# Mixture of experts on tokens sorted by expert: row tiles of 128 with indirect scatter and gather in place of all experts on all tokens

## Chip, cores and metric

The kernel runs on one core of a Trainium2 chip. The metric is the device time of one execution in microseconds; the time given is the median of three runs.

## What is computed

The input is 16 sequences of 256 tokens, 128 wide, in f32. Four stages follow one another, each on the layer-normalised output of the one before, each with a residual: attention a (causal, 8 heads, a geometric term in the scores), experts (called B), attention b (16 heads, not causal), and the experts again (called D, with the same weights). The experts:

```python
logits = einsum('bsd,ed->bse', tgt, Wr) + br          # 8 experts
top_v, top_i = top_k(logits, 2)
top_w = softmax(top_v)
router_w = sum(one_hot(top_i, 8) * top_w[..., None], axis=-2)
h = relu(einsum('bsd,efd->bsef', tgt, W1) + b1)       # F = 512
o = einsum('bsef,edf->bsed', h, W2) + b2
tgt2 = einsum('bsed,bse->bsd', o, router_w)
return layer_norm(tgt + tgt2, gamma, beta)
```

Only two of the eight weights of a token are not zero.

## The kernel before

The 4096 tokens are cut into 8 groups of 512 (two sequences, four tiles of 128 tokens). For each group there is one stage of each kind: A (attention a), B (experts), C (attention b), D (experts). The program is unrolled in Python. `attention` returns a list of steps, small functions that each issue a few instructions; `experts` returns another.

An attention normalises its group (`layernorm`, with DVE statistics and a power step on POOL, L179 and L180), turns it (`transposed`, L191), projects q and k (L230) and v (L245), then goes through units of four heads and one sequence. A unit computes scores with the queries on the partitions (`maxima`, L265), takes the row maxima on DVE (L275, L280), turns them (`shift`, L291), computes the scores again with the keys on the partitions (`weights`, L309), takes the exponential on ACT (L319), and multiplies with v (`weighted`, L328). The heads of a unit lie on 32 partitions each, so the score matmuls use 32 rows of the PE array each.

An expert stage normalises and turns its group into `tgtT` (128 x 512). `route` computes the logits (L427) and the two weights of each token. `spread` turns the weights, writes them to DRAM and reads them back onto every partition (L481, L485). Then all 8 experts run on all 512 tokens: `up` (L497) makes one quarter of the hidden layer, 128 x 512 in PSUM, ACT or DVE applies bias and relu (L506, L504), and `down` (L513) adds four such quarters up. DVE multiplies an expert's output with its weights (L522), and POOL adds it to the sum (L527). `end` turns the sum back (L532), `end2` normalises, scales and adds the residual on POOL (L541 to L547). The weights of all experts are loaded once at the start (16 loads of 256 KB) and stay.

Two streams of stages are interleaved in the program: A0, A1, C0, A2, C1 and so on, and B0, B1, D0, B2, D1 and so on. A stage opens when the stage before it on the same group is done. The attention stream goes ahead while it is at most 1.25 stages in front. So except at both ends an attention always has an expert stage of another group beside it. A scheduler below the program assigns buffers and orders the instructions of each engine, with the order in the program as priority; the engines then run their queues in order. All loads and stores go through SP's queue.

Of the kernel before, what the change touches and what calls it, by code (L numbers as in the profile page):

```python
# [9 lines left out]
F32 = mybir.dt.float32  # L10
AF = mybir.ActivationFunctionType
# [6 lines left out]
T = 256          # tokens of one batch element  # L18
C = 128          # model width
G = 512          # tokens of one group: two batch elements  # L20
NT = G // P      # token tiles of a group
HA, DA = 8, 16   # heads and head width of the first attention
HB, DB = 16, 8   # and of the second
E, F = 8, 512    # experts and their hidden width
NF = F // P
EB = 4          # experts whose token weights are spread in one load
EPS = 1e-5
NEG = -1e30
# columns of the constants
C_DD, C_ID, C_KA, C_KB, C_DESC, C_N = 0, 256, 512, 513, 514, 522  # L30
# [3 lines left out]
def block_kernel(  # L34
    ctx: ExitStack,
    tc: tile.TileContext,
    x: bass.AP,        # [tokens, C]
    wqT_a: bass.AP,    # [C out, C in]
    wk_a: bass.AP,     # [C in, C out]
    wv_a: bass.AP,     # [C in, C out]  # L40
    wo_a: bass.AP,     # [C in, C out]
    hs: bass.AP,       # [C, 1] head scale of each q column
    wq_b: bass.AP,     # [C in, C out]
    wk_b: bass.AP,
    wv_b: bass.AP,
    wr: bass.AP,       # [C, E]
    br: bass.AP,       # [E]
    w1: bass.AP,       # [C, E, F]
    b1: bass.AP,       # [P, E, NF]
    w2: bass.AP,       # [P, E, NF, C]  # L50
    b2: bass.AP,       # [C, E]
    gamma: bass.AP,    # [C]
    beta: bass.AP,     # [C]
    cst: bass.AP,      # [P, C_N]
    out: bass.AP,      # [tokens, C]
# [37 lines left out]
    b1_sb = loaded("b1_sb", b1)  # L93
    b2_sb = loaded("b2_sb", b2)
    w1_sb, w2_sb = [], []
    for e in range(E):
        w1_sb.append(loaded(f"w1_{e}", w1[:, e, :]))
        w2_sb.append(loaded(f"w2_{e}", w2[:, e, :, :]))
# [20 lines left out]
    )  # L119
    mhalf = const.tile([P, NT], F32, name="mhalf")  # L120
    nc.gpsimd.memset(mhalf, -0.5)

    # Each head takes 32 partitions of q^T and k^T, so that four heads lie in the four row
    # groups of the PE array. The row behind a head's own is 1 in k^T, and takes minus the
    # row maximum of the scores in q^T.
    # first attention: q' = q (scale I + head_scale d d^T), folded into its weights
# [22 lines left out]
    # v with a column of ones behind each head's, for the row sums  # L149
# [9 lines left out]
    # minus the row maxima, token-major, one column of 32 for a head  # L159
# [10 lines left out]
    def layernorm(src, dst, n):  # L170
        """dst = (src - mean) / sqrt(var + eps) over the last axis of [P, NT, C]."""
        st = small.tile([P, NT, 6], F32, tag="st", name=f"st_{n}")
        mv = small.tile([P, NT, 2], F32, tag="mv", name=f"mv_{n}")
        for t in range(NT):
            nc.vector.bn_stats(st[:, t, :], src[:, t, :])
        for t in range(NT):
            nc.vector.bn_aggr(mv[:, t, :], st[:, t, :])
        r = small.tile([P, NT], F32, tag="lnr", name=f"lnr_{n}")
        nc.gpsimd.tensor_scalar(r, mv[:, :, 1], EPS, None, ALU.add)  # L179
        nc.gpsimd.tensor_tensor(r, r, mhalf, ALU.pow)  # L180
        for t in range(NT):
            nc.vector.tensor_scalar(
                dst[:, t, :], src[:, t, :], mv[:, t, 0:1], r[:, t:t + 1],
                ALU.subtract, ALU.mult,
            )

    def transposed(src, dst, n):
        """[P tokens, NT, C] -> [C, G]"""
# [5 lines left out]
    def mask_diagonals(ps, mask):  # L194
        """The blocks at columns 0 and 256 of both heads are on the diagonal."""
# [8 lines left out]
    def attention(kind, g):  # L204
        """The steps of an attention and its residual on group g."""
# [48 lines left out]
        def maxima(bb, quad, pair, u):  # L254
            """Scores with the queries on the partitions, for their row maxima."""
# [4 lines left out]
            # (query tile, columns, keys)  # L260
# [25 lines left out]
        def shift(bb, quad, u):  # L286
            """q^T with minus the row maxima behind each head."""
# [11 lines left out]
        def weights(bb, quad, pair, u):  # L299
            """exp(scores - maxima) with the keys on the partitions."""  # L300
# [3 lines left out]
            # (key tile, columns, first query)  # L304
# [17 lines left out]
        def weighted(bb, quad, u):  # L322
            """(weights v)^T, and their sums behind each head."""
# [85 lines left out]
    def experts(n, g, last):  # L409
        """The steps of the mixture of experts, its norm and its residual on group g."""  # L410
        s = {}

        def start():
            tgt = work.tile([P, NT, C], F32, tag="tgt", name=f"tgt_{n}")
            layernorm(xg[g], tgt, n)
            s["tgt"] = tgt

        def start2():
            tgtT = work.tile([P, G], F32, tag="tgtT", name=f"tgtT_{n}")
            transposed(s["tgt"], tgtT, n)  # L420
            s["tgtT"] = tgtT

        def route():
            """The weights of the two best experts of each token; the first of equals wins."""
            ps = ps_mm.tile([P, NT, E], F32, tag="mm", name=f"lg_{n}")
# [6 lines left out]
            desc = cst_sb[:, C_DESC:C_DESC + E].unsqueeze(1).to_broadcast(shape)  # L432

            def best(lg, i):
                m = small.tile([P, NT], F32, tag=f"rm{i}", name=f"rm{i}_{n}")
                nc.vector.tensor_reduce(m, lg, axis=AX.X, op=ALU.max)
                eq = small.tile(shape, F32, tag="req", name=f"req{i}_{n}")
# [4 lines left out]
                k = small.tile([P, NT], F32, tag="rk", name=f"rk{i}_{n}")  # L442
                nc.vector.tensor_reduce(k, eq, axis=AX.X, op=ALU.max)
                one = small.tile(shape, F32, tag=f"rone{i}", name=f"rone{i}_{n}")
# [5 lines left out]
            lg = small.tile(shape, F32, tag="rl", name=f"rl_{n}")  # L450
# [3 lines left out]
            m1, one1 = best(lg, 1)  # L454
            lg2 = small.tile(shape, F32, tag="rl2", name=f"rl2_{n}")
# [3 lines left out]
            m2, one2 = best(lg2, 2)  # L459
            ex = small.tile([P, NT], F32, tag="rex", name=f"rex_{n}")  # L460
            nc.vector.tensor_tensor(ex, m2, m1, ALU.subtract)
            nc.scalar.activation(ex, ex, AF.Exp)
            wa = small.tile([P, NT], F32, tag="rwa", name=f"rwa_{n}")
            nc.vector.tensor_scalar(wa, ex, 1.0, None, ALU.add)
            nc.vector.reciprocal(wa, wa)
            wb = small.tile([P, NT], F32, tag="rwb", name=f"rwb_{n}")
            nc.vector.tensor_tensor(wb, ex, wa, ALU.mult)
            w = small.tile([P, E, NT], F32, tag="rw", name=f"rw_{n}")
            nc.vector.tensor_tensor(one1, one1, wa.unsqueeze(2).to_broadcast(shape), ALU.mult)
            nc.vector.tensor_tensor(one2, one2, wb.unsqueeze(2).to_broadcast(shape), ALU.mult)  # L470
            nc.vector.tensor_tensor(w.rearrange("p e t -> p t e"), one1, one2, ALU.add)
            s["w"] = w

        def spread():
            """The weights with the tokens on the free axis, on every partition."""
            ps = ps_mm.tile([E * NT, P], F32, tag="mm", name=f"wt_{n}")
            nc.tensor.transpose(ps, s["w"].rearrange("p e t -> p (e t)"), ident)
            wT = small.tile([E * NT, P], F32, tag="wT", name=f"wT_{n}")
            nc.vector.tensor_copy(wT, ps)
            wd = dpool.tile([E * NT, P], F32, tag="wd", name=f"wd_{n}")  # L480
            nc.sync.dma_start(out=wd, in_=wT)  # L481
            s["wbc"] = []
            for i in range(E // EB):
                wbc = work.tile([P, EB, G], F32, tag="wbc", name=f"wbc_{n}_{i}", bufs=3)
                nc.sync.dma_start(  # L485
                    out=wbc.rearrange("p e k -> p (e k)"),
                    in_=wd[i * EB * NT:(i + 1) * EB * NT, :]
                    .rearrange("a b -> (a b)").partition_broadcast(P),
                )
                s["wbc"].append(wbc)  # L490

        hs_ = {}

        def up(i):
            e, f = divmod(i, NF)
            ps = ps_h.tile([P, G], F32, tag="h", name=f"h_{n}_{i}")
            nc.tensor.matmul(  # L497
                ps, lhsT=w1_sb[e][:, f * P:(f + 1) * P], rhs=s["tgtT"],
                start=True, stop=True,
            )  # L500
            hT = work.tile([P, G], F32, tag="hT", name=f"hT_{n}_{i}", bufs=4)
            bias = b1_sb[:, e, f:f + 1]
            if f == NF - 1:
                nc.vector.tensor_scalar(hT, ps, bias, 0.0, ALU.add, ALU.max)  # L504
            else:
                nc.scalar.activation(hT, ps, AF.Relu, bias=bias)  # L506
            hs_[i] = hT

        def down(i):
            e, f = divmod(i, NF)  # L510
            if f == 0:
                s["o"] = ps_mm.tile([P, G], F32, tag="mm", name=f"o_{n}_{e}")
            nc.tensor.matmul(  # L513
                s["o"], lhsT=w2_sb[e][:, f, :], rhs=hs_.pop(i),
                start=(f == 0), stop=(f == NF - 1),
            )
            if f < NF - 1:
                return
            if e == 0:
# [148 lines left out]
```

## Time and profile before

| | |
|---|---|
| median of 3 runs | 1953.25 us (1953.03 to 1953.45) |
| profiled execution, first to last instruction | 1953.5 us |
| granted TensorE clock, mean | 0.903 |
| busy: PE, DVE, ACT, POOL | 1775.6, 824.6, 494.1, 279.3 us |
| HBM read, written | 40.73 MB, 2.36 MB |
| DMA queue of SP | 43.10 MB, 6.0% of 16 engines' span |

The page of the profile gives each engine's busy time and its share of the span, a strip of 40 equal slices, the DMA queues, the chain of work that ended last, and the costliest groups of instructions. A group's line has the source line, the engine, the operation, output and inputs, shapes, the count, busy time in us and the mean ns of one, then the idle time of the engine ahead of these instructions and what ended it. Matmuls overlap in the records, so the mean duration of one is longer than the distance from one start to the next. PE's clock is given as a share of full speed. The chain that ended last is 85% PE, 7% DVE and 7% POOL.

### The profile page before, as it was taken

The numbers are of one execution on the slowest core, as the hardware profiler recorded it, in microseconds if no ns is written. First come the engines' busy times: TensorE is split into PE (matmuls) and PEld (weight loads), VectorE is DVE, ScalarE is ACT, GpSimd is POOL, SyncE is SP. The second block draws the span as 40 slices with busy tenths as digits, with TensorE's granted clock in tenths as the row PEclk, the third lists the DMA queues.
The fourth block names the chain that finished last, engine by engine and source line by source line (L and its number), as shares of the span: only waits on it lengthen the run. The fifth ranks groups of instructions, "written<-read, shape, count | busy, mean of one in ns | idle before, by whom it ended". The sixth has DMA issues, their size and how long they took to land.

```text
span 1953.5 us, 19448 instructions
## 1 busy us (share of the span) xinstructions
PE 1775.6 (91%) x7794; PEld 848.6 (43%) x7794; DVE 824.6 (42%) x1912; ACT 494.1 (25%) x705; POOL 279.3 (14%) x293
## 2 busy tenths in 40 slices
PE   7896998989989899798998989899998989969977
PEld 4443444444444444344444434444444444434433
DVE  5444335453354533545335453454435453243232
ACT  1130231313313133131322223132231313303311
POOL 1012002120121201212011110211102120120122
PEclk7697898999979799798998989899897999979978
DMA  4010100101010010101001010010100101001010
GB/s 148 1 43 1 44 1 0 44 6 44 1 44 1 6 44 1 44 1 49 2 1 44 1 49 1 1 44 1 49 1 1 44 6 44 1 1 44 1 49 5
DMA packets 18377, 44.33 MB, mean 23 GB/s; under 512 B 2160, under 2 KB 12016, under 8 KB 14192
## 3 DMA queue, kind: packets, MB, share of 16 engines
q1 hardware_dynamic: 18288, 43.10, 6.0%
q8 instruction: 61, 1.00, 0.2%
q14 instruction: 28, 0.23, 0.0%
HBM read 40.73 MB, written 2.36 MB: 22 GB/s over the span
## 4 chain that ended last, share of the span: by engine, by line
PE 85%; DVE 7%; POOL 7%; issue 1%; SPq 0%; DMA 0%; POOLq 0%; ACT 0%; DVEq 0%
PE h_B L497 13%; PE o_B L513 13%; PE h_D L497 12%; PE o_D L513 11%; PE st_b L309 7%; PE s_b L265 7%; PE av_b L328 4%; PE pj_b L230 3%; PE st_a L309 3%; PE s_a L265 2%; PE pj_a L230 2%; PE av_a L328 2%; POOL x L547 1%; PE ot_b L372 1%; PE lg_D L427 1%
## 5 line engine op out<-in xcount | busy, mean ns | idle before, releaser
L497 PE MATMUL h_B<-tgtT_B,w 128*128 128x512 f32 x512 | 288.5, 654 | 0.2 <-DVE tgtT_B L192 0.2
L497 PE MATMUL h_D<-tgtT_D,w 128*128 128x512 f32 x512 | 283.2, 646 | 0.0
L513 PE MATMUL o_B<-hT_B,w 128*128 128x512 f32 x512 | 273.1, 619 | 0.0
L513 PE MATMUL o_D<-hT_D,w 128*128 128x512 f32 x512 | 267.9, 608 | 0.0
L506 ACT ACTIVATE hT_D<-h_D,b_sb 128x512 f32<-128x512 f32 x192 | 131.9, 687 | 477.4 <-PE h_D L497 464.5
L280 DVE TENSOR_REDUCE mtok_b<-s_b 128x4 f32<-128x1024 f32 x128 | 156.6, 1225 | 193.6 <-PE s_b L265 193.4
L506 ACT ACTIVATE hT_B<-h_B,b_sb 128x512 f32<-128x512 f32 x192 | 131.9, 687 | 407.3 <-PE h_B L497 401.8
L319 ACT ACTIVATE pT_b<-st_b 128x1024 f32<-128x1024 f32 x128 | 131.0, 1023 | 267.1 <-PE st_b L309 267.1
L265 PE MATMUL s_b<-qk_b 32*128 32x256 f32 x1024 | 168.1, 431 | 1.8 <-DVE mtok_b L280 1.8
L527 POOL TENSOR_TENSOR acc_B<-acc_B,oe_B 128x512 f32<-128x512 f32 x56 | 70.8, 1265 | 645.3 <-DVE oe_B L522 632.8
L309 PE MATMUL st_b<-qm_b,qk_b 32*128 32x256 f32 x1024 | 163.0, 424 | 0.0
L527 POOL TENSOR_TENSOR acc_D<-acc_D,oe_D 128x512 f32<-128x512 f32 x56 | 70.8, 1265 | 596.3 <-DVE oe_D L522 596.3
L497 PEld LDWEIGHTS h_D<-tgtT_D,w 128*128 128x128 f32 x512 | 95.6, 203 | 106.2 <-issue 87.8
L497 PEld LDWEIGHTS h_B<-tgtT_B,w 128*128 128x128 f32 x512 | 92.3, 201 | 108.8 <-issue 97.7
L265 PEld LDWEIGHTS s_b<-qk_b 32*128 32x128 f32 x1024 | 96.4, 198 | 93.7 <-issue 76.2
L309 PEld LDWEIGHTS st_b<-qm_b,qk_b 32*128 32x128 f32 x1024 | 93.0, 193 | 78.7 <-issue 59.6
L513 PEld LDWEIGHTS o_D<-hT_D,w 128*128 128x128 f32 x512 | 86.8, 189 | 83.2 <-issue 77.7
L513 PEld LDWEIGHTS o_B<-hT_B,w 128*128 128x128 f32 x512 | 83.1, 189 | 84.3 <-issue 82.5
L504 DVE TENSOR_SCALAR hT_B<-h_B,b_sb 128x512 f32<-128x512 f32 x64 | 48.0, 751 | 169.7 <-PE h_B L497 169.5
L265 PE MATMUL s_a<-qk_a 32*128 32x128 f32 (+1 forms) x512 | 76.5, 421 | 25.0 <-DVE mtok_a L275 25.0
L504 DVE TENSOR_SCALAR hT_D<-h_D,b_sb 128x512 f32<-128x512 f32 x64 | 48.1, 751 | 99.8 <-PE h_D L497 99.8
L197 DVE TENSOR_TENSOR st_a<-st_a,cmaskT 128x512 f32<-128x512 f32 x64 | 44.7, 699 | 81.7 <-PE st_a L309 80.1
(242 smaller groups left out, 1617.8 us busy)
## 6 DMA issues: line engine op xcount, KB each, us to landing
wbc_B<-wd_B SPq DMA_DIRECT2D x16, 1024.0 KB, 5.9
wbc_D<-wd_D SPq DMA_DIRECT2D x16, 1024.0 KB, 5.6
w<-in_w_dram SPq DMA_DIRECT2D x16, 256.0 KB, 5.5
x<-in_x_dram SPq DMA_DIRECT2D x8, 256.0 KB, 3.9
out_dram<-x SPq DMA_DIRECT2D x8, 256.0 KB, 2.3
cst_sb<-in_cst_dram SPq DMA_DIRECT2D x1, 261.0 KB, 3.1
wd_B<-wT_B SPq DMA_DIRECT2D x8, 16.0 KB, 1.4
wd_D<-wT_D SPq DMA_DIRECT2D x8, 16.0 KB, 1.4
```

Source lines behind the costliest of these rows:

```text
L197: nc.vector.tensor_tensor(dg, dg, mask.unsqueeze(1).unsqueeze(1).to_broadcast([P, 2, 2, P]), ALU.add)
L230: nc.tensor.matmul(ps, lhsT=wqk[:, which, quad * P:(quad + 1) * P], rhs=s["xnT"], start=True, stop=True,)
L265: nc.tensor.matmul(ps[:, j, col:col + nk], lhsT=qT[r:r + 32, o + t * P:o + (t + 1) * P], rhs=kT[r:r + 32, o:o + nk], start=True, stop=True,)
L280: nc.vector.tensor_reduce(m[:, :, heads, d:d + 1].rearrange("p t j s -> p j t s"), ps.rearrange("p j (t k) -> p j t k", k=T), axis=AX.X, o ...
L309: nc.tensor.matmul(ps[:, j, col:col + T - q0], lhsT=kT[r:r + 32, o + t * P:o + (t + 1) * P], rhs=qm[r:r + 32, q0:T], start=True, stop=True,)
L319: nc.scalar.activation(pT[:, :, 0:w], ps[:, :, 0:w], AF.Exp)
L328: nc.tensor.matmul(ps[32 * j:32 * j + 32, q0:T], lhsT=va[:, 2 * bb + t, quad * 4 + j, :], rhs=u[f"pT{j // 2}"][:, j % 2, t * T:t * T + T - ...
L497: nc.tensor.matmul(ps, lhsT=w1_sb[e][:, f * P:(f + 1) * P], rhs=s["tgtT"], start=True, stop=True,)
L504: nc.vector.tensor_scalar(hT, ps, bias, 0.0, ALU.add, ALU.max)
L506: nc.scalar.activation(hT, ps, AF.Relu, bias=bias)
L513: nc.tensor.matmul(s["o"], lhsT=w2_sb[e][:, f, :], rhs=hs_.pop(i), start=(f == 0), stop=(f == NF - 1),)
L527: nc.gpsimd.tensor_tensor(s["acc"], s["acc"], to, ALU.add)
```

## The change

The expert layer is rebuilt around a sort. Its new parts:

- `prepare` (norm, turning and routing of one group) now belongs to the attention stream, behind the attention of the same group. It keeps the one-hot choices and the two weights for a chunk of four groups (`CG`), 2048 tokens. `spread` is gone.
- `dispatch`, once per chunk: three small matmuls count the tokens of each expert ahead of each token, some twenty DVE operations make a row number for each choice of each token (every expert's rows start at a multiple of 128) and the expert of each of 39 tiles (`NE` = 2 x 16 + 8 - 1, the most that can be needed). Then 32 indirect DMAs on POOL scatter the normalised rows into a DRAM buffer, 128 rows of 512 bytes each.
- `tiles`, once per chunk: the 39 tiles run in batches of four. SP reads four expert numbers into registers and loads each tile's expert weights (128 x 1156 f32, 592 KB) at that offset, into six buffers; it loads four tiles of rows; PE turns them; `up` and `down` run with 128 columns. Rows of a tile without tokens are computed too. The output, with its bias, goes to a second DRAM buffer.
- `combine`, once per group: 8 indirect DMAs on POOL gather the two output rows of each token, DVE multiplies and adds, and the norm and residual follow as before.
- The resident expert weights and biases are gone; W1, W2, b2 and b1 lie behind one another in one input, `we`. The constants grow by triangular and index matrices. Two row buffers in DRAM are filled with zeros at the start.
- The order: the attention stream is a0 to a7 and then b0 to b7, each with its `prepare` behind it. The expert stream is, for B and then D, and for each of two chunks: `dispatch`, `tiles`, four `combine`. A dispatch opens when the last group of its chunk is prepared; b of a group opens when its B is combined. The two streams are now paced by costs in ns that are written at the steps, the expert stream's times 1.5.

The core of the diff:

```diff
+CG = 4
+CT = CG * NT
+NE = 2 * CT + E - 1
+TB = 4
...
+        def scatter(t):
+            for k in range(2):
+                i = nc.gpsimd.indirect_dma_start(
+                    out=ch["xs"], out_offset=bass.IndirectOffsetOnAxis(
+                        ap=ch["idx"][:, k, t:t + 1], axis=0),
+                    in_=ch["tgt"][t // NT][:, t % NT, :], in_offset=None,
+                    bounds_check=NE * P - 1, oob_is_err=False,
+                )
...
+        def load(b):
+            k = min(TB, NE - b * TB)
+            regs = nc.values_load_multi_w_load_instructions(
+                ch["ti"][0:1, b * TB:b * TB + k], engines=[mybir.EngineType.SP],
...
+            for j in range(k):
+                w = work.tile([P, W_N], F32, tag="we", name=f"we_{n}_{b * TB + j}", bufs=6)
                 nc.sync.dma_start(
+                    out=w,
+                    in_=we[bass.ds(regs[j], 1), :, :].rearrange("a p w -> (a p) w"),
+                )
...
         def up(i):
...
+            ps = ps_h.tile([P, NF, P], F32, tag="h", name=f"h_{n}_{i}")
+            hT = work.tile([P, NF, P], F32, tag="hT", name=f"hT_{n}_{i}", bufs=3)
+            for f in range(NF):
+                nc.tensor.matmul(
+                    ps[:, f, :], lhsT=w[:, f * P:(f + 1) * P],
+                    rhs=s[f"xT{b}"][:, j * P:(j + 1) * P], start=True, stop=True,
+                )
...
         def down(i):
...
+            for f in range(NF):
+                nc.tensor.matmul(
+                    ps, lhsT=hT[:, f, :], rhs=w[:, W_2 + f * C:W_2 + (f + 1) * C],
+                    start=(f == 0), stop=(f == NF - 1),
+                )
...
+            nc.vector.tensor_tensor(s["o4"][:, j, :], ps, w[:, W_B2:W_B2 + C], ALU.add)
...
+        steps = [(lambda: load(0), 0), (lambda: rows(0), 0), (lambda: turn(0), 450)]
+        for i in range(NE + 1):
+            b, j = divmod(i, TB)
+            if j == 0 and b + 1 < NB:
+                steps += [(lambda b=b: load(b + 1), 0), (lambda b=b: rows(b + 1), 0)]
+            if i < NE:
+                steps.append((lambda i=i: up(i), 860))
+            if i > 0:
+                steps.append((lambda i=i: down(i - 1), 860))
+            if j == 1 and b + 1 < NB:
+                steps.append((lambda b=b: turn(b + 1), 450))
...
+        def gather():
+            s["r"] = []
+            for k in range(2):
+                r = work.tile([P, NT, C], F32, tag=f"r{k}", name=f"r{k}_{n}{g}")
+                for t in range(NT):
+                    nc.gpsimd.indirect_dma_start(
+                        out=r[:, t, :], out_offset=None, in_=ch["os"],
+                        in_offset=bass.IndirectOffsetOnAxis(
+                            ap=ch["idx"][:, k, q * NT + t:q * NT + t + 1], axis=0),
...
+    att, ffn = [], []
+    for kind, n in (("a", "B"), ("b", "D")):
+        for g in range(NG):
+            cost = 35000 if kind == "a" else 65000
+            att.append((f"{kind}{g}", f"D{g}" if False else (f"B{g}" if kind == "b" else None),
+                        lambda kind=kind, g=g: attention(kind, g), cost))
+            att.append((f"p{n}{g}", None, lambda n=n, g=g: prepared(n, g), None))
+    for n in "BD":
+        for c in range(NCH):
+            last_g = (c + 1) * CG - 1
+            ffn.append((f"d{n}{c}", f"p{n}{last_g}", lambda n=n, c=c: dispatch(f"{n}{c}", chunks[n, c]), None))
+            ffn.append((f"t{n}{c}", None, lambda n=n, c=c: tiles(f"{n}{c}", chunks[n, c]), None))
+            for g in range(c * CG, (c + 1) * CG):
+                ffn.append((f"{n}{g}", None, lambda n=n, c=c, g=g: combine(n, g, chunks[n, c], n == "D"), None))
...
+    PACE = 1.5
     while sa.open() or sf.open():
-        if sa.open() and (not sf.open() or sa.at() <= sf.at() + SHIFT):
-            sa.step()
+        if not sf.open():
+            sf.clock = max(sf.clock, sa.clock)
+        if not sa.open():
+            sa.clock = max(sa.clock, sf.clock)
+        if sa.open() and (not sf.open() or sa.clock <= sf.clock):
+            sa.step(1.0)
         else:
-            sf.step()
+            sf.step(PACE)
```

## Prediction

> **What bounds the kernel now.** I read the page's busy shares, then the costliest groups, then windows of engine busy time (columns: stretch, length, busy time and count of PE, weight loads, DVE, ACT, POOL, then PE's granted clock, DMA share, GB/s), then PE's timeline (start, length, instruction).
>
> ```profile
> PE 1775.6 (91%) x7794; PEld 848.6 (43%) x7794; DVE 824.6 (42%) x1912; ACT 494.1 (25%) x705; POOL 279.3 (14%) x293
> ...
> L497 PE MATMUL h_B<-tgtT_B,w 128*128 128x512 f32 x512 | 288.5, 654 | 0.2 <-DVE tgtT_B L192 0.2
> L513 PE MATMUL o_B<-hT_B,w 128*128 128x512 f32 x512 | 273.1, 619 | 0.0
> ```
>
> PE is the bound, at 91%; nothing else passes 42%. The expert matmuls are half of its work: 2048 instructions of 512 columns, each f32 product being two instructions (64 products of a group and layer stand as 128).
>
> ```profile
> 50.00:60.00 10.00, 9.94 (x48) 6.11 (x50) 3.65 (x10) 2.71 (x4) 0.00 (x0) 0.50 0.01 2
> 200.00:210.00 10.00, 10.00 (x30) 5.70 (x31) 4.38 (x21) 3.25 (x5) 0.00 (x0) 0.51 0.01 2
> 340.00:400.00 60.00, 59.38 (x275) 27.50 (x272) 26.55 (x60) 19.54 (x29) 6.37 (x7) 1.00 0.10 36
> ```
>
> These three decide my forecast. At 50 to 60 us the first attention runs alone: PE is busy, yet at half clock. At 200 to 210 the second attention has hardly a full-array matmul beside it: half clock again. At 340 to 400 attention and experts alternate: full clock. So attention alone, with its matmuls on 32 of 128 rows, costs PE double.
>
> ```profile
> 406.07 1.05 PE L245 MATMUL v_b<-wv_b_sb,xnT_b 128*128 128x128 f32 x8
> 406.96 1.02 PE L513 MATMUL o_D<-hT_D,w 128*128 128x512 f32 x2
> ...
> 358.59 0.92 PE L309 MATMUL st_a<-qm_a,qk_a 32*128 32x256 f32 x8
> 359.44 1.12 PE L513 MATMUL o_D<-hT_D,w 128*128 128x512 f32 x2
> ```
>
> Start to start at full clock: eight 128x128 instructions take 0.89 us, so an f32 product of 128 columns takes 0.222 us. A 128x512 one takes 0.858 (1898.69 to 1899.54). Short matmuls cost in proportion to their columns; weight loads stay hidden.
>
> **What the Trainium skill says.** "TensorE: Matmul & The Clock Gate", Part 1, says that PE runs at half clock unless recently active. The trace agrees on 0.50 and 1.00, but shows that "active" isn't mere occupation: 9.94 of 10 us busy, at 0.50. "DMA: Bandwidth & Descriptors", Issuing engine by pattern, gives indirect transfers to GPSIMD, and its Anatomy of one DMA puts a fixed cost of about 2.0 us on a transfer from there; no run here shows one. "Perfetto Trace Analysis", DMA Instruction — SWDGE, says that such an instruction is shown until its descriptors are generated, not until its data lands; also unseen here.
>
> **The change part by part.** I count PE work at full clock ("full-clock us"), then ask at which clock it runs.
>
> Per group, attention a: 64 score and 64 weight instructions at 0.86 per 8 (13.7), av 4 x 0.79 (3.2), projections 8 x 0.43 (3.4), the rest some 45 at 0.11 to 0.14 (5.4): 26. Attention b: 128 + 128 at 1.06 per 8 (34), av 8 x 1.13 (9), projections 16 x 0.43 (6.9), 44 others (5): 55. Eight groups: 648.
>
> Removed: 1024 expert products x 0.858 = 879 full-clock us, and per expert stage the spread and the last transposes (some 1 us). Check: 648 + 879 + routers and transposes 16 x 2.2 = 1562; over the mean clock 0.903 that is 1730, against 1775.6 busy.
>
> Added on PE: the tile count is fixed, whatever the routing: 39 tiles of 128 rows for each of 2 chunks of 2 layers, 156. Each has 8 products: 1248 x 0.222 = 277; turning rows 156 x 0.11 = 17; routers 16 x 2 = 32. So PE's work falls from 1562 to 974.
>
> Beside PE: DVE loses relu and weighting (96 + 96 us) and small things (25), and gains per tile a relu (0.35, scaled from 0.75 at 512), a bias add (0.29), a quarter of a 0.69 copy: 0.81 x 156 = 126, and 38 for combining: about 790. ACT falls: 468 relus at 0.37 (172) for 264. Both stay hidden. Start: 4 MB of weights no longer load ahead; the first attention didn't wait for them: nothing. The zero fill of 5 MB is due only 250 us later: nothing; uncovered, 14 us at 380 GB/s.
>
> SP: every tile now loads its expert's 592 KB, and moves 64 KB in and 64 KB out: 720 KB, at the 380 GB/s of 12 to 20 us 1.9 us. Beside attention a tile takes over 3 us, so this is hidden; alone, PE's 1.89 us and DMA's 1.9 are level, and with register reads and six weight buffers I take 2.2 (1.9 to 3.0). In SP's queue the loads wait for weight buffers; behind them stand row loads and stores, for which PE's turning and the gathers wait; whatever attention matmuls stand behind a turning in PE's queue wait with it (I price that as slip in the range, 0 to 100 us).
>
> POOL: 112 adds of 1.265 us go (142). 256 indirect transfers come: 32 scatters and 32 gathers for each chunk. Unseen: the smallest POOL row (0.23 us, L179) and the page's 2.0 us bound it; descriptors for 128 rows could double that. I take 1.5 and keep 0.5 to 4. No gain is possible, since each is added work. Behind them in POOL's queue stand the norms' power steps, for which DVE and then PE wait.
>
> The order is what costs. All a come before all b, and a chunk starts only after four groups' routers:
>
> 1. a0 to a3 have nothing beside them. Before, the lone a0 took 56 us (12 to 68) at half clock; with its router 60. Four and 10 at the start: 250.
> 2. a4 to a7 with chunk one. Ranks and slots (8), 32 scatters (48) and landing take 60, a4 alone meanwhile (56). Then 39 tiles (74) and a5 to a7 (78) with routers (8) are 160 at about 0.9: 180. Together 240.
> 3. b0 to b3 with chunk two. For 60 us of scattering b runs alone; a b alone is 100 (55 at half clock, less what its projections gain), so 0.6 of one. The pacing weighs a chunk at (39 x 1720 + 10 x 450) x 1.5 = 107,000 and a b at 65,000: 1.65 b pass per chunk: (91 + 74)/0.97 = 170. The remaining 1.75 b alone: 175. Sum 405.
> 4. b4 to b7 with the third chunk: the same, 405.
> 5. The last chunk, with nothing beside it: norm and router 18 (as 1865 to 1887 now, less the matmuls between), slots 8, scatters 48, landing and turning 5, tiles 39 x 2.2 = 86; then gathers 32 x 1.5 = 48, four groups' POOL steps of 5.1 between them 20, last norm and store 10: 243.
>
> Sum: 250 + 240 + 405 + 405 + 243 = 1543; I say 1545, 0.79 of the profiled span of 1953.5, which is the 1953.25 median within 0.3. The stall that vanishes is PE queuing for experts; what is late next is PE's clock in lone attention, and at the end POOL's queue.
>
> **The rivals.** Full clock everywhere: if short matmuls keep PE warm and lone attention is warmed too, 974/0.95 + head, stalls and what the last chunk adds besides its matmuls (181) = 1206. Against it: both half-clock windows. For it: warmth after b's projections (0.81 at 190 to 200).
>
> Indirect transfers dear: at 4 us the last chunk gains 64 x 2.5 = 160 and each earlier chunk starts 80 later, of which attention hides most, say 30 in all: 1735. Against it: only a power-step-like software dispatch is sure. For it: nothing priced here generates 128 addresses.
>
> Slower: half clock throughout. If the 128-column bursts, with relus and buffer waits between, don't lift the clock in the mixed stretches either, all 974 run at 0.5: 1948 + 181 = 2130. It decides below a mean clock of 974/(1953 - 181) = 0.55; mine is 974/(1545 - 181) = 0.71. For it: 0.59 over the first attention, although that has projections. Against it: 1.00 in the mix at 340, with about the same half share of full-array work.
>
> That the experts aren't reduced isn't possible: tiles are counted in the program. That weights bind in mixed stretches isn't likely either: 39 x 720 KB at half the rate is 148 us, under their 180 to 405.
>
> **How the numbers follow.** Forecast 0.66, dear transfers 0.16, full clock 0.10, slower 0.07, no difference 0.01. Unknowns about the forecast: transfers at 0.5 us, -64; a lone b at 75, -118; tiles alone -12 to +31; queues that wait in an order foreseen wrongly, up to +100; transfers at 4 us, +190. Taking these not all at once, 1380 to 1760. That leaves out full clock, slower and the dearest transfers, 2 in 10. Faster by over 0.2% 0.92, within 0.2% (about what a measurement of this kernel can tell from no change) 0.01, slower 0.07.
>
> **What would show it.** Windows over a0 to a3, and over b with no tiles beside it: clock near 0.5, 56 and about 100 us per group. Mixed stretches: clock above 0.9. Eight tile matmul instructions start to start: 0.89. POOL's rows for scatter and gather: about 1.5 us. After the last attention matmul some 240 us without any. I am wrong if lone b runs at full clock, if tiles run at half, if an indirect transfer costs over 3 us, or if PE idles long in the middle behind the scatters.

## The result, and the profile after

The changed kernel takes 1967.88 us (median of 4 runs, 1963.74 to 1973.05) against 1953.14 us beside it: a ratio of 1.0074, with a 95% interval of 1.0057 to 1.0091. It is slower by 0.7%, where I had forecast 1545 us. The profiled execution has a span of 1966.2 us.

The page after, for the rows shown of before: busy shares, then PE's busy tenths and its granted clock in 40 slices, and four groups (busy time, mean ns, then the idle time before them and what ended it).

```profile
PE 1366.8 (70%) x8350; PEld 878.0 (45%) x8350; DVE 800.5 (41%) x2125; ACT 367.8 (19%) x789; POOL 398.5 (20%) x438
...
PE   7788834998509169994499893599954898943840
...
PEclk7555556999755579996566655799965666556975
...
L310 PE MATMUL st_b<-qm_b,qk_b 32*128 32x256 f32 x1024 | 192.4, 521 | 75.1 <-DVE mtok_b L281 72.6
...
L608 PE MATMUL h_B<-xT_B,we_B 128*128 128x128 f32 x624 | 94.4, 288 | 0.8 <-issue 0.8
L663 POOL DMA_INDIRECT r_D<-os,didx_D x64 | 67.8, 1059 | 120.5 <-DMA os<-o_D 104.5
L625 PE MATMUL o_B<-we_B,hT_B 128*128 128x128 f32 x624 | 91.3, 288 | 0.0
```

The work did shrink: PE is busy for 1366.8 us in place of 1775.6, which is 409 less. But span less busy time, PE's idleness, went from 177.9 us (1953.5 - 1775.6) to 599.4, which is 421 more. The two cancel. The holes stand in the strip of tenths: 0 and 1 in slices where it was 9. The clock strip shows the rest of what is wrong: 9 only where tiles run, 5 to 7 elsewhere (mean 0.704, before 0.903).

Windows of the kernel after (columns as in those of before):

```profile
650.00:700.00 50.00, 4.09 (x16) 3.64 (x16) 7.56 (x36) 0.20 (x1) 29.35 (x30) 0.50 0.29 109
...
800.00:850.00 50.00, 46.50 (x346) 34.79 (x343) 26.54 (x72) 14.85 (x39) 3.14 (x5) 1.00 0.47 139
900.00:950.00 50.00, 15.15 (x80) 7.25 (x78) 19.09 (x68) 3.09 (x5) 42.31 (x42) 0.50 0.14 39
...
1100.00:1150.00 50.00, 47.00 (x229) 22.52 (x227) 16.42 (x19) 9.31 (x11) 0.00 (x0) 0.60 0.00 1
...
1750.00:1800.00 50.00, 1.12 (x4) 0.72 (x4) 3.86 (x16) 0.00 (x0) 31.29 (x32) 0.50 0.37 129
1800.00:1850.00 50.00, 42.67 (x351) 42.48 (x352) 14.36 (x46) 18.59 (x63) 0.00 (x0) 0.90 0.80 264
```

At 650 and at 1750 POOL works on 30 and 32 instructions, the scatters, and PE does next to nothing. At 800 tiles and attention are mixed: full clock. At 900 the gathers run on POOL and PE is again mostly idle. At 1100 a group of b runs alone, busy for 94% at a clock of 0.60; at 1800 tiles run alone, busy for only 85% at 0.90. So being busy isn't what tells these stretches apart. They differ in their matmuls, on 32 rows in attention's scores and on 128 in tiles; that the rows decide is read from such windows, as no run changed them.

PE's timeline at the first scatter (start, length, instruction; in brackets the idle time before it and what ended it):

```profile
271.52 0.43 PE L496 MATMUL dr_B<-cst_sb,dtot_B 128*128 128x8 f32 x2
320.34 1.12 PE L597 MATMUL xt_B<-ident,x_B 128*128 128x128 f32 x4 [48.39 <-DMA x_B<-xs]
321.25 1.06 PE L192 MATMUL tp_a<-ident,xn_a 128*128 128x128 f32 x4
```

After the ranks (`dr_B`) the next instruction in PE's queue is the first turning of sorted rows (`turn(0)`, L597), which needs all 32 scatters. The next attention's transposes (`tp_a`) had nothing to wait for, but stand behind it: 48.4 us without a matmul. The same wait begins again at 658.3, 1204.2 and 1750.0, so once for each chunk.

Then the gathers. VectorE's timeline around them, the kernel after:

```profile
519.26 0.42 DVE L365 TENSOR_TENSOR x<-y_a,x 128x256 f32<-128x256 f32 x1 [0.80 <-PE y_a L360]
...
572.62 0.25 DVE L176 BATCH_NORM_STATS2 st_B<-x 128x6 f32<-128x128 f32 x1
...
583.53 2.05 DVE L183 TENSOR_SCALAR tgt_B<-x,mv_B,lnr_B 128x128 f32<-128x128 f32 x4 [2.56 <-POOL lnr_B L181]
```

```profile
584.95 1.15 PE L192 MATMUL tp_B<-ident,tgt_B 128*128 128x128 f32 x4 [65.73 <-DVE tgt_B L183]
```

The attention of group a6 is done at 519.68 (`x`). Its norm's statistics (`st_B`) start only at 572.62: combining steps that wait for gathered rows stand ahead of them in VectorE's queue, and the norm's power step (L181) stands behind the same 32 gathers in POOL's. PE, third in line (`tp_B`), idles for 65.7 us, and a7 runs alone after that. The gathers take some 42 us of POOL's queue here (32 at 1.30), the combining's own steps on POOL some 20 (5.1 for each of four groups). In the stretches of b it is the row maxima (`mtok_b`, L281) that stand behind the combining, for 17.6 + 13.8 + 10.2 = 42 us in each (the first and the third of these are 55.7 of the 72.6 us before `st_b` in the page's groups).

### The profile page after: what moved, and what is told of

It is laid out like the page before. It is cut to its first block, busy times and chain, and to the rows that moved or that the text cites. A ratio compares the mean times of both kernels' runs of the same rounds, so it can differ in the third digit from the quotient of the medians.

```text
span 1966.2 us, 22137 instructions
## 1 busy us (share of the span) xinstructions
PE 1366.8 (70%) x8350; PEld 878.0 (45%) x8350; DVE 800.5 (41%) x2125; ACT 367.8 (19%) x789; POOL 398.5 (20%) x438
## 4 chain that ended last, share of the span: by engine, by line
PE 56%; issue 19%; POOL 10%; DVE 10%; DMA 2%; ACT 1%; SPq 1%; POOLq 0%; DVEq 0%; ACTq 0%
PE st_b L310 8%; PE av_b L329 6%; PE s_b L266 6%; PE o_D L625 4%; PE h_D L608 4%; PE st_a L310 3%; PE pj_b L231 3%; PE s_a L266 3%; PE av_a L329 3%; PE h_B L608 3%; PE o_B L625 2%; POOL r_B L663 2%; DVE mtok_b L281 2%; POOL r_D L663 2%; PE pj_a L231 2%
## 5 line engine op out<-in xcount | busy, mean ns | idle before, releaser
L310 PE MATMUL st_b<-qm_b,qk_b 32*128 32x256 f32 x1024 | 192.4, 521 | 75.1 <-DVE mtok_b L281 72.6
L281 DVE TENSOR_REDUCE mtok_b<-s_b 128x4 f32<-128x1024 f32 x128 | 153.5, 1219 | 152.8 <-PE s_b L266 152.3
L382 POOL TENSOR_TENSOR x<-on_b,x 128x256 f32<-128x256 f32 x16 | 11.6, 724 | 814.9 <-DVE on_b L377 814.9
L329 PE MATMUL av_b<-pT_b,vaug_b 128*32 128x256 f32 x1024 | 150.3, 536 | 3.5 <-ACT pT_b L320 3.5
L310 PE MATMUL st_a<-qm_a,qk_a 32*128 32x128 f32 (+1 forms) x512 | 97.6, 486 | 2.8 <-DVE mtok_a L276 2.7
L608 PE MATMUL h_B<-xT_B,we_B 128*128 128x128 f32 x624 | 94.4, 288 | 0.8 <-issue 0.8
L625 PE MATMUL o_B<-we_B,hT_B 128*128 128x128 f32 x624 | 91.3, 288 | 0.0
L608 PEld LDWEIGHTS h_B<-xT_B,we_B 128*128 128x128 f32 x624 | 80.7, 195 | 22.6 <-issue 20.6
L608 PE MATMUL h_D<-xT_D,we_D 128*128 128x128 f32 x624 | 89.9, 286 | 0.8 <-DVE xT_D L599 0.8
L597 PE MATMUL xt_D<-ident,x_D 128*128 128x128 f32 x78 | 14.0, 307 | 109.7 <-DMA x_D<-xs 109.7
L625 PE MATMUL o_D<-we_D,hT_D 128*128 128x128 f32 x624 | 88.0, 286 | 1.1 <-DVE o_D L631 1.1
L625 PEld LDWEIGHTS o_B<-we_B,hT_B 128*128 128x128 f32 x624 | 79.0, 195 | 21.4 <-issue 12.3
L266 PE MATMUL s_a<-qk_a 32*128 32x256 f32 (+1 forms) x512 | 79.4, 433 | 10.3 <-DVE mtok_a L276 10.3
L608 PEld LDWEIGHTS h_D<-xT_D,we_D 128*128 128x128 f32 x624 | 80.1, 198 | 13.6 <-issue 11.5
```

Of the source, the lines that this page charges most:

```text
L266: nc.tensor.matmul(ps[:, j, col:col + nk], lhsT=qT[r:r + 32, o + t * P:o + (t + 1) * P], rhs=kT[r:r + 32, o:o + nk], start=True, stop=True,)
L281: nc.vector.tensor_reduce(m[:, :, heads, d:d + 1].rearrange("p t j s -> p j t s"), ps.rearrange("p j (t k) -> p j t k", k=T), axis=AX.X, o ...
L310: nc.tensor.matmul(ps[:, j, col:col + T - q0], lhsT=kT[r:r + 32, o + t * P:o + (t + 1) * P], rhs=qm[r:r + 32, q0:T], start=True, stop=True,)
L329: nc.tensor.matmul(ps[32 * j:32 * j + 32, q0:T], lhsT=va[:, 2 * bb + t, quad * 4 + j, :], rhs=u[f"pT{j // 2}"][:, j % 2, t * T:t * T + T - ...
L382: nc.gpsimd.tensor_tensor(xs, on, xs, ALU.add)
L597: nc.tensor.transpose(ps[:, j * P:(j + 1) * P], s["x4"][:, j, :], ident)
```

## The experiments

Theory (queues): each wait above is the head of an in-order queue that holds up work whose inputs are ready; let that work pass, and the time comes back. Rival (chain): the transfers are themselves on the way to the end, and order gains nothing. Later a third reason came up, PE's clock in lone attention.

**turn_later.** Attention's steps are put between the scatters and the first turning (the larger buffer lets attention go that far ahead):

```
-            (lambda t=t: scatter(t), 0) for t in range(CT)
+            (lambda t=t: scatter(t), 1400) for t in range(CT)
...
-            tgt = work.tile([P, NT, C], F32, tag="tgt", name=f"tgt_{n}{g}", bufs=CG + 2)
+            tgt = work.tile([P, NT, C], F32, tag="tgt", name=f"tgt_{n}{g}", bufs=8)
```

> Each scatter step counts 1400 ns in the pacing, so that about one attention pass over a group stands ahead of the chunk's first turning of rows in PE's queue; tgt gets 8 buffers for 6, since more groups are prepared before a chunk is combined. Queue theory (the time went where PE's next attention matmuls stand behind a turning that waits for scattered rows): three of the four PE gaps of 48 us close, the last one has no attention left to fill it; 1968 - 145 = 1825, within 1795 to 1850. Chain theory (the tiles need the rows anyway, and the end follows from them): the chunk only starts as late as before and ends as late, 1950 to 1975.

Measured: 1815.13 us, ratio 0.928 [0.921, 0.935]. Of PE's four waits of 48 us, three are gone but for 8 us of one; the last (48.3 us, nothing beside it) and those at the gathers (59, 40 and 40 us) are not. PE's timeline at the same place as above:

```profile
270.82 0.43 PE L496 MATMUL dr_B<-cst_sb,dtot_B 128*128 128x8 f32 x2
271.11 1.09 PE L192 MATMUL tp_a<-ident,xn_a 128*128 128x128 f32 x4
```

153 us for three waits of 48 (145): the queue theory holds, the chain theory falls. The larger buffer isn't the reason: gathers_spaced has it too, and there all four waits stay at 48 us.

**gathers_spaced.** The gathers of a group are issued one by one, 700 ns apart in the pacing, and a group is combined only after the next group's gathers (`tgt` has 8 buffers here too; the part of the edit in the order of the streams isn't shown):

```
-        return [(gather, 0), (end, 0), (end2, 0)]
+        gathers = [
+            (lambda t=t, k=k: gather(t, k), 700) for t in range(NT) for k in range(2)
+        ]
+        return gathers, [(end, 0), (end2, 0)]
```

> The gathers are issued one by one with 700 ns each in the pacing, and the combining of a group stands behind the gathers of the next one. Queue theory: the 66 us gap in which a norm's power step stands behind 32 gathers on POOL, and the two sets of gaps of 42 us in which the row maxima stand behind the combining on DVE, shrink to some 8 us each: 1968 - 130 = 1838, within 1810 to 1870; the wait at the scatters stays. Chain theory: attention waits for POOL's sum of work all the same, 1950 to 1975.

Measured: 1875.28 us, ratio 0.960 [0.955, 0.965]. The 66 us fell to 7.4 + 4.3, each 42 to some 23 (9.9 + 7.4 + 6.6; 8.2 + 7.7 + 6.1), and a new wait of 10 came. The way is right, the size just outside what I had set: 93 us in place of 130. The waits at the scatters stay (48.1 to 48.3 us).

**both.** The two edits together.

> The two edits together. Queue theory: the two savings add up, 1968 - 275 = 1693, within 1650 to 1750, and so the change is faster than the kernel before by about 13%. Chain theory: above 1930.

Measured: 1774.57 us, ratio 0.911 [0.904, 0.918]: 193 us gained where 246 would be the sum of the parts. A wait that was hidden behind another came out, at the seam of the layers:

```profile
544.64 1.15 PE L192 MATMUL tp_B<-ident,tgt_B 128*128 128x128 f32 x4 [12.87 <-DVE tgt_B L183]
...
569.34 1.15 PE L192 MATMUL tp_b<-ident,xn_b 128*128 128x128 f32 x4 [20.89 <-DVE xn_b L183]
```

The first group of b needs the first combined group, so the gathers are on its path here, and pacing can't hide them.

**direct.** What the indirect transfers cost with all that hangs on them: every scatter and gather is a plain copy of SP's queue. The rows aren't sorted then, so this kernel leaves out a part of the computation.

```
-                i = nc.gpsimd.indirect_dma_start(
-                    out=ch["xs"], out_offset=bass.IndirectOffsetOnAxis(
...
+                at = (k * CT + t) * P
+                i = nc.sync.dma_start(
+                    out=ch["xs"][at:at + P, :], in_=ch["tgt"][t // NT][:, t % NT, :])
...
```

> Scatter and gather are left out: plain copies of the same bytes on SP's queue take their places, so that rows are not sorted and what is computed is not the reference's; tile count, weight loads and order are those of the changed kernel. Queue theory: the gaps at scatters and gathers go, and the tail loses its 48 us of scatters and some 40 of gathers as well: 1968 - 145 - 130 - 85 = 1610, within 1560 to 1680. If the gaps came from something else in the dispatch (the small DVE steps, the register reads, weight loads) they stay and the time is above 1850.

Measured: 1632.59 us, ratio 0.836 [0.827, 0.845]; no wait of PE over 7.2 us. So of the changed kernel's time some 335 us belong to the indirect transfers and the queues behind them (the four runs lie between 1617.58 and 1649.67 us).

**both_spread and direct_spread.** What is left is the clock. The tiles of the two chunks beside attention b last over four groups in place of some two (in the direct kernel, which gets the larger buffer too, at 3.1 and 3.5, and 1.8 for the first chunk):

```
-    PACE = 1.5
+    PACE = {'tB1': 2.5, 'tD0': 3.0}
...
-            sf.step(PACE)
+            sf.step(PACE.get(sf.stages[sf.k][0], 1.5))
```

> Both reorderings of queues as before, and the 39 tiles of the chunks that lie beside b0 to b3 and b4 to b7 are paced to last over the four groups of attention and not over some two of them. Clock theory: attention alone runs at about 0.6 of the full clock (100 to 109 us a group) and tiles beside it lift the clock to over 0.9, so that each of the two stages of b loses some 70 us: 1774 - 140 = 1635 us, range 1590 to 1690, with a mean granted clock over 0.78. Chain theory: a group of b takes its 100 us by its own chain of small steps whatever the clock is, so spreading gains nothing: over 1740 us and a clock that stays near 0.74.

> As the kernel with plain copies in place of the indirect transfers (rows are not sorted, so the output is not the reference's), with the tiles of the first chunks paced to last over their four groups. No indirect transfer disturbs the order here. Clock theory: the stretch from a4 to the last b (about 1210 us at a mean clock of 0.81) goes at about 0.92, so 1632 us becomes 1510, range 1460 to 1560. Chain theory: no gain, 1600 to 1660 us.

Measured: 1737.62 us (ratio 0.888 [0.887, 0.890]) and 1544.84 us (0.789 [0.787, 0.791]). Run again beside others, the first took 1736.61. Spreading gained 88 us where nothing else disturbs, within what the clock theory had set, but only 37 with the indirect transfers: both_spread and its clock (0.755 in the median run, where over 0.78 was expected) came out nearer to the rival's figures. Two windows of both_spread tell why:

```profile
950.00:1000.00 50.00, 29.78 (x138) 14.30 (x136) 17.61 (x63) 5.42 (x8) 41.10 (x41) 0.53 0.16 42
...
1250.00:1350.00 100.00, 88.36 (x634) 57.09 (x636) 44.76 (x101) 28.76 (x58) 3.12 (x5) 0.90 0.28 82
```

With ten tiles to a group of b (1250) the clock is 0.90 in place of 0.60: the clock theory holds, and with direct_spread's 88 us the rival, under which a group of b takes its time whatever the clock, falls. But tiles that end with the fourth group push their gathers to its end (950), and there the old wait is back. Each expected number that took both gains together was too good.

**plain_gathers** splits the 193 us between those two: from both_spread, the gathers alone become plain copies. Its first runs were disturbed, of which more below; plain_gathers_2 is the same kernel on the chip of both_spread.

> As the kernel with both reorderings and spread tiles (1737.6 us), the scatters indirect as there, the gathers plain copies of SP's queue (the combined rows are the wrong ones, so the output is not the reference's). It splits the 193 us that lie between that kernel and the one with plain copies throughout (1544.8). Queue theory: the waits at the gathers (12.6, 20.9 and 6.4 us ahead of b0, 8.7 and 15.0 in b3, 22.1 and 19.5 ahead of the last dispatch) and 36 us of the tail go, less some 25 that stay: 1737 - 115 = 1620 us, range 1580 to 1665. Rival, that the rest lies with the scatters or with the clock: over 1690 us.

> The kernel of plain_gathers once more. If the waits belong to the program, 1712 us within 12 and the waits again; if they belong to the set and are gone, 1620 us (1580 to 1665) as the queue theory said, since some 80 us of TensorE's gaps lie at them.

Measured: 1712.33 us, and in the undisturbed set 1626.62 us, against 1736.61 for both_spread in that set. So the gathers and what waits behind them are worth 110 us even in the better order. The remaining 82 us (1626.62 - 1544.84) are in the main the scatters: the last still stops PE for 49 us, and the plain copies also need not wait for slots. direct_spread has neither of the two reorderings and another pacing, so the figure isn't that of the scatters alone.

**half_spread.** Chunks of two groups in place of four (`CG = 2`), both reorderings, tiles spread over their two groups (pace 1.15 and 2.3 in place of 1.5).

> Both reorderings of queues, chunks of two groups in place of four (23 tiles each, 184 in all in place of 156, as each chunk has seven tiles for uneven experts), tiles paced to last over their two groups. If the lone head and tail and the lone groups of b are what is left of the loss: two lone groups of a at the start in place of four (saves about 60 us), 23 tiles and half the gathers after the last scatter (saves about 80), 28 tiles more (costs about 65), the spreading as in the other kernel (saves about 140): 1774 - 215 = 1560 us, range 1500 to 1640. If what is left is work and not order, the added tiles tell: 1800 us or more.

Measured: 1720.73 us, ratio 0.879 [0.877, 0.881], and 1719.51 when run again. The lone head is shorter by two groups of a, but PE does 8858 instructions in place of 8350, and every chunk has its scatters: 17 us better than both_spread, where I had expected 1560.

**half_last.** Of half_spread, only the last chunk's scatter is put ahead of the gathers of the chunk before it.

> As the kernel with chunks of two groups and spread tiles (1720.7 us), the norms left on POOL; alone the last chunk's scatter stands ahead of the gathers of the chunk before it, whose combining comes behind the last tiles. Queue theory: the last gap of PE, 56.2 us, becomes 29, as it did with the norms moved, and the tail stays within some 5 us of 42.6: 1720 - 27 = 1693 us, range 1675 to 1710. Rival, that the gathers only move to the end and are paid there: 1710 to 1730.

PE's line at the last scatter, in half_spread (in half_spread_2, the same kernel, the wait is 56.1 us) and in half_last_2, half_last's kernel as run beside half_spread_2:

```profile
1627.48 1.11 PE L597 MATMUL xt_D<-ident,x_D 128*128 128x128 f32 x4 [56.21 <-DMA x_D<-xs]
```

```profile
1607.92 1.11 PE L597 MATMUL xt_D<-ident,x_D 128*128 128x128 f32 x4 [29.58 <-DMA x_D<-xs]
```

Measured: 1739.89 us, and 1727.67 beside the 1719.51 us of half_spread_2. The wait halved just as expected, but from the last group's transposes to the end half_last_2's trace has 158 us, half_spread_2's 166: of the 27 us, 18 were paid behind the scatter (new waits of 8.9 and 6.3 us), mostly as the rival had it. Ahead of that the two issue the same instructions and differ by 15 us all the same, and the runs of the one (1702.79 to 1733.43 us) and the other (1711.92 to 1739.11) overlap, so 9 us can't be told from none.

**norm_off_pool and half_best.** The norms' power step leaves POOL for ScalarE, as exp(-0.5 ln(v)), and attention's residual (L382) goes to VectorE. norm_off_pool is both_spread with this edit, half_best is half_last with it.

```
-        nc.gpsimd.tensor_scalar(r, mv[:, :, 1], EPS, None, ALU.add)
-        nc.gpsimd.tensor_tensor(r, r, mhalf, ALU.pow)
+        nc.scalar.activation(r, mv[:, :, 1], AF.Ln, bias=eps_sb)
+        nc.scalar.activation(r, r, AF.Exp, scale=-0.5)
...
```

> As the kernel with both reorderings and spread tiles (1737.6 us), but the power step of every norm is done on ScalarE as the exponential of a logarithm, and the residual's addition of attention (L382) on VectorE, so that POOL's queue holds the transfers and the end of the combining, and nothing that attention waits for. Queue theory: the waits of 8.7 and 15.0 us in b3, of 22.1 and 19.5 us ahead of the last dispatch and of 12.6 and 20.9 us ahead of b0 shrink by some 60 in all; 1737 becomes 1680 us, range 1640 to 1710. Rival, that VectorE's combining steps, which stand in its queue until their rows have come, hold attention just as much: no gain, 1720 to 1760.

> As the kernel with chunks of two groups (1720.7 us), with the same two steps taken off POOL, and the last chunk's scatter put ahead of the gathers of the chunk before it, whose combining comes behind the last tiles. Queue theory: the last scatter's PE gap of 56.2 us falls to some 30, as 16 scatters take 21 us and no gathers stand ahead; the smaller waits shrink by 20: 1720 becomes 1675 us, range 1640 to 1700. Rival: what remains is work at a low clock and not waiting: 1705 to 1740.

> The kernel of norm_off_pool once more; its trace showed 66 loads of ScalarE's function tables, 1.28 us each and 85 us in all[...]. Queue theory with the loads hidden: 1680 us, range 1640 to 1715. Rival, that the loads stand in attention's path (two for each of 32 norms, and those of the 32 groups of attention's halves wait for them): 1740 to 1800.

Measured: 1823.56 us, the second time 1806.60, and 1779.49 us for half_best: all slower than what they started from. ScalarE's groups in norm_off_pool_2 (count, busy time, mean ns):

```profile
L180 ACT ACT_TABLE_LOAD x33 | 42.3, 1283 | 5.4 <-DVE mv_a L178 4.8
...
L181 ACT ACT_TABLE_LOAD x33 | 42.3, 1283 | 0.6
```

Each norm loads two tables: 85 us on ScalarE. The Trainium skill's "ScalarE activation tables: per-element evaluation and per-set limits", What a function is on this engine, puts two functions of different sets one load of 1283 ns apart. The trace agrees to the nanosecond on a load, and its two loads per norm show that logarithm and exponential came from different sets here; I hadn't priced that. As these runs were disturbed too, whether the loads alone took the gain isn't settled.

**gathers_wide.** Tiles paced at 2.0 and 2.3, their gathers at 2.0 and 2.4.

> As both_spread (1737 us), with the tiles of the second and third chunk paced at 2.0 and 2.3 in place of 2.5 and 3.0, and their gathers at 2.0 and 2.4 in place of 1.5, so that gathers have room to pass between attention's norms before the last group ends. Queue theory: of the waits at gathers in b3 and ahead of the last dispatch (24 and 44 us) some 45 go, and a group of b with fewer tiles beside it gives back some 15: 1737 - 30 = 1707 us, range 1685 to 1730. Rival, that the time is PE's clock alone: the tiles that are drawn closer cost 10 to 30 us more, 1745 to 1770.

Measured: 1819.28 us, but with TensorE's stalls (below), which cost plain_gathers 86 us: inconclusive. Less 86, it would lie near both_spread.

**The disturbance.** In norm_off_pool (both times), half_best, half_last, plain_gathers and gathers_wide other engines wait for TensorE's results while scatters run, and no TensorE instruction in the trace ends those waits (the view of waits writes "remote"). In plain_gathers, at its first scatter:

```profile
ACT pT_a L320 <- DVE st_a L198: 46.3, 3, 24.4
DVE st_a L198 <- remote: 21.1, 2, 12.9
```

I ran four kernels side by side to see whether this belongs to the programs.

> The kernel of both_spread once more, side by side with plain_gathers. If the unexplained waits of TensorE beside the scatters belong to the program, 1738 us within 10 and no such waits; if they belong to the set of runs, 1770 us or more with them, or all four kernels of this set without them.

> The kernel of half_spread once more. Program: 1721 us within 10 and no such waits. Set of runs: 1750 us or more with them, or without them if none of this set has them.

> The kernel of half_last once more. Program: 1740 us within 10 and the waits again. Set of runs, and this set without them: 1693 us (1675 to 1710), as the queue theory said.

None of the four had such waits, plain_gathers_2 and half_last_2 included. So it isn't the program alone. The experiments ran on five chips: on two of them none of eight traces with a scatter beside attention shows it, on the other three all six do. Each of these three was used for one set of runs, so the chip and the time of the runs can't be told apart, and what it is stays open. It was seen only in kernels with a scatter beside attention; the kernel before has no scatter, and ran alike everywhere (1953 to 1956 us).

## Why the prediction was wrong

The step that failed is the order in time, in steps 2 to 4: "a4 alone meanwhile" and "For 60 us of scattering b runs alone". I had taken the stream that lists attention and experts side by side for two streams that run side by side. Each engine has one queue, filled in program order, and a step of cost zero goes into it at once. I did name the attention matmuls behind a turning and the norms' power steps behind the transfers, but the order in time has nothing for either, and "queues that wait in an order foreseen wrongly" were priced at up to +100; the trace has 3 x 48 = 145 us at the scatters and 66 + 42 + 42 = 150 at the gathers.

By the prediction's own steps:

1. a0 to a3: 250, measured 262. Right: 62 to 63 us a group, clock 0.51 to 0.57.
2. a4 to a7 with chunk one: 240, measured 387 (262 to 649). 48.4 + 65.7 are the two waits. The mix took 199 us (320 to 519) in place of 180, and a7 was left to run alone after the gathers.
3. b0 to b3: 405, measured 546 (649 to 1195). 48.1 + 42 are waits; no part of a b ran beside the scatter, so that part ran alone later, and a lone b took 106 to 109 us in place of 100. The mix took 186 for 170.
4. b4 to b7: 405, measured 545, in the same way.
5. The last chunk: 243, measured 226. Right in the main: PE waits 48.4 at the scatters, tiles take 96 (1798 to 1894) in place of 86, and 71.6 us follow PE's last instruction, in place of 78.

The differences are +12, +147, +141, +140 and -17: 423, which is the whole error (1966 - 1543). Of it 295 are the named waits. The other 128 lie in slower mixed stretches and in more and slower lone groups, as the steps say; no run takes these apart. turn_later and gathers_spaced gave 153 and 93 of it back, both 193.

What was right: PE's clock, alone and mixed, and so the mean (0.704, forecast 0.71); a tile's eight instructions 0.89 us start to start; DVE's 800.5 us (forecast 790, although the terms listed add up to 772); the tail. My mean clock came true by other means, though: I had some 1364 us of PE's work (974/0.71) and 181 of anything else, the trace has PE busy for 1366.8 and idle for 599. So the work was foreseen, and the idleness wasn't; "if PE idles long in the middle behind the scatters" was the last sign named of being wrong, and it is the one that came. Of the others, a lone b ran at 0.60 and tiles at 0.90 or more, as forecast. An indirect transfer was cheaper than taken: 0.98 us (scatter) or 1.00 us (gather) with 0.30 between in an undisturbed row, so 1.28 to 1.30 from start to start, in place of 1.5. So "dear transfers" fell as a rival in price and came true in effect: not their length but what stands behind them costs. "Full clock everywhere" and "half clock throughout" fell; the end on the other side, slower, came by neither rival but by the waits.

That direct_spread takes 1544.8 us is chance: it has no indirect transfers, and spreads tiles as I hadn't assumed. It does show that the smaller work is worth some 400 us once no indirect transfer stands in its way. The best kernel with the full computation, half_spread, keeps 234 us of that, 12% of the time before: 1720 us against 1954.

## What to carry to other kernels

Before trusting that two streams overlap, write down for each engine what its queue holds right behind each instruction that waits for a long transfer: the price of a wait is the work behind it, not the transfer. A step of no cost in a list scheduler isn't free; it decides who stands behind whom. And when work is removed, look whether the clock was high only beside it: here TensorE, 94% busy with attention alone, ran at 0.60, and at 0.90 with tiles spread over it.

## What the runs showed that I had not expected

- 32 indirect transfers of 128 rows of 512 bytes take POOL 41 us, 1.28 us each, most of it (0.98) within the instruction. The Trainium skill's "DMA: Bandwidth & Descriptors", Anatomy of one DMA, has some 2.0 us of fixed cost for a transfer from there, setup and completion together. In a row, POOL is free for the next after 1.28, so that figure isn't what each transfer of a row holds POOL for.
- In the runs on three chips TensorE stalled beside scatters: in plain_gathers 24 us at the first of them, and 86 us in all (1712.33 against 1626.62 for the same kernel on another chip). Such kernels are safely compared only side by side on one chip.
